# Four graph-attention layers on 128 graphs: score columns become rows by DMA through DRAM instead of by TensorE transposes

## The chip, the cores and the metric

The kernel runs on one core of a Trainium2 chip, as one launch. A core has a matrix engine (TensorE; PE in the profile, with PEld for its weight loads), three engines for elementwise work (VectorE: DVE; ScalarE: ACT; GpSimd: POOL), and a sync engine (SP) that in this kernel issues every DMA. The metric is the device time of one execution in microseconds, lower is better; the median of several executions is compared.

## What is computed

128 independent graphs of 128 nodes with 512 features each go through four graph-attention layers. Each layer first normalizes (layer norm, then ReLU), and adds its result to its input. Cut to what matters:

```python
h = relu(layernorm(x))
# layer 0: scores f1_i + f2_j, f = (h W^T) a;   attention over j of h itself; elu
# layer 1: GAT, 4 heads of 256, x W1, softmax over sources; elu; then a second
#          GAT of 1 head on the 1024 features, W2;            + bias b2
# layer 2: scores h.w_src_i + h.w_dst_j + b;    attention over j of h itself
# layer 3: 8 heads of 64, x W_proj, scores a_src_i + a_dst_j + b;  relu
x = x + layer(h)
# in every layer and head:
e[i, j] = leaky_relu(own[i] + other[j], 0.2)      # masked where adj has no edge
att     = softmax(e)
```

So a graph has five attentions with 1, 4, 1, 1 and 8 heads: 15 score matrices of 128 x 128. Each is the sum of a column (`own`, one value per partition) and of a row (`other`, one value per free position). Both are computed as columns, with nodes on the partitions, so `other` has to be turned into a row that every partition holds.

## The kernel before, in words

All is float32. Weights are loaded once and stay in SBUF (`w1x`, `w2x`, `wpx`: the projection weights with the score vectors folded in as leading columns, lines 85 to 94 and 129 to 171; pool `setup` holds what only this preparation needs). Then each graph is a Python generator, `graph` (L422), which makes three masks from the adjacency, runs `layer0` to `layer3` one after the other, and stores its 128 x 512 tile `xt`. Every `yield` is a place where the next graph may come in. The loop at L445 keeps up to FLYING = 7 graphs in flight, steps each of them by one yield per turn, and starts a new graph every APART = 11 turns at the earliest. A graph before the change has 71 turns. The input of a graph is loaded two graphs ahead (`loaded`, L411).

The kernel is written for a tile framework. It places the waits between engines, and it also decides in which order the instructions of different graphs stand on an engine: this order is near the program's, with exceptions, and is fixed when the program is built. Each engine takes its own list in that order. In the built programs, one pitch of this list (one graph starts, one ends, all seven in flight advance) repeats unchanged through the middle of the run.

The pieces the change and the prediction touch:

- `norm_relu` (L177): `bn_stats` and `bn_aggr` on DVE (L180, L182), epsilon and the power -0.5 on POOL (L185, L187), `nmr` on DVE (L190), and `h` on ACT (L192). Four times a graph.
- `dot` (L196): score columns of layers 0 and 2, one DVE instruction of 128 x 512 for each.
- `projected` (L278): matmuls of `ht` or `y` against a weight, in column parts, each part copied from PSUM by ACT (L293). The score columns are the first columns of the first part.
- `transposed` (L210): TensorE transposes, four to a bank (L217), copied out by ACT (L219).
- `attention` (L223): for each head a TensorE transpose of the `other` column, broadcast to 128 columns, into PSUM (L233): this is the row on all partitions. Then on DVE, for each head, row plus mask with the maximum along the row (L240), the shift (`neg`, `nm`), the addition of `own` (L257 or L259) and the leaky ReLU (L262); on ACT the exponential with its sum, one instruction for each head (L266); on DVE the reciprocal `rz` (L275).
- `applied` (L295): transpose of the weights, and one matmul of 128 x 512 (L299).
- The multi-head attentions have their own matmuls (L337 with output `po`, L393 with output `pa`). The transposed mask of layer 1 is a TensorE transpose too (L433).

SP carries, before the change, only loads of `xt` and of adjacencies (one for four graphs) and the stores of results, L415, L419 and L439.

Of the kernel before, what the change touches and what calls it, by code (L numbers as in the profile page):

```python
# [8 lines left out]
F32 = mybir.dt.float32  # L9
I32 = mybir.dt.int32  # L10
AF = mybir.ActivationFunctionType
ALU = mybir.AluOpType
# [4 lines left out]
LOWEST = -3.0e38  # L17
SLOPE = 0.2
EPS = 1e-5
FLYING = 7  # L20
APART = 11
AHEAD = 2

# [2 lines left out]
def kernel(  # L26
# [23 lines left out]
    nc = tc.nc  # L50
    B, P, D = x.shape
    KC = D // P
    H1, F1 = l1_src1.shape
    HF = H1 * F1
    FC = HF // P
    H3 = l3_watt.shape[0]
# [2 lines left out]


    const = ctx.enter_context(tc.tile_pool(name="const", bufs=1))
    adjp = ctx.enter_context(tc.tile_pool(name="adjp", bufs=3))
    xpool = ctx.enter_context(tc.tile_pool(name="xpool", bufs=FLYING + AHEAD))
    masks = ctx.enter_context(tc.tile_pool(name="masks", bufs=FLYING))
    big = ctx.enter_context(tc.tile_pool(name="big", bufs=2))
    mid = ctx.enter_context(tc.tile_pool(name="mid", bufs=3))
    small = ctx.enter_context(tc.tile_pool(name="small", bufs=8))
    ps = ctx.enter_context(tc.tile_pool(name="ps", bufs=8, space=PSUM))

    def bank(name):  # L70
        return ps.tile([P, 512], F32, tag="bank", name=name)
# [40 lines left out]
    with tc.tile_pool(name="setup", bufs=1) as st:  # L112
# [47 lines left out]
        for c in range(KC):  # L160
            for s in range(2):
# [8 lines left out]
                    wpx[:, c, s * H3 : (s + 1) * H3], prod, AX.X, ALU.add  # L170
                )

# [44 lines left out]
        yield  # L220
        return r

    def attention(own, other, mask, nh, tag):  # L223


        e = (big if nh > 4 else mid).tile([P, nh, P], F32, tag=tag, name=tag)
        mx = small.tile([P, nh], F32, tag=f"mx{nh}", name="mx")
        for g in range(0, nh, 4):
            m = min(4, nh - g)
            pb = bank("pb")  # L230
            for j in range(m):

                nc.tensor.transpose(  # L233
                    pb[:, j * P : (j + 1) * P],
                    other[:, g + j : g + j + 1].to_broadcast([P, P]),
                    ident,
                )
            yield
            for j in range(m):
                nc.vector.tensor_tensor_reduce(  # L240
                    out=e[:, g + j, :],
                    in0=pb[:, j * P : (j + 1) * P],
                    in1=mask,
                    scale=1.0,
                    scalar=LOWEST,
                    op0=ALU.add,
                    op1=ALU.max,
                    accum_out=mx[:, g + j : g + j + 1],
                )

        neg = small.tile([P, nh], F32, tag=f"neg{nh}", name="neg")
        nc.vector.scalar_tensor_tensor(neg, mx, -1.0, own, ALU.mult, ALU.subtract)
        nm = small.tile([P, nh], F32, tag=f"nm{nh}", name="nm")
        nc.vector.scalar_tensor_tensor(nm, neg, SLOPE, neg, ALU.mult, ALU.min)
        ef = e.rearrange("p h q -> p (h q)")
        if nh == 1:
            nc.vector.tensor_scalar(ef, ef, own, None, ALU.add)  # L257
        else:
            nc.vector.tensor_tensor(  # L259
                e, e, own.unsqueeze(2).to_broadcast([P, nh, P]), ALU.add  # L260
            )
        nc.vector.scalar_tensor_tensor(ef, ef, SLOPE, ef, ALU.mult, ALU.max)  # L262
        yield
        z = small.tile([P, nh], F32, tag=f"z{nh}", name="z")
        for j in range(nh):
            nc.scalar.activation(  # L266
                e[:, j, :],
                e[:, j, :],
                AF.Exp,
                bias=nm[:, j : j + 1],  # L270
                accum_out=z[:, j : j + 1],
            )
        yield
        rz = small.tile([P, nh], F32, tag=f"rz{nh}", name="rz")
        nc.vector.reciprocal(rz, z)  # L275
        return e, rz

    def projected(lhs, n_k, w, parts, to):  # L278

        width = w.shape[2] // parts  # L280
        for lo in range(0, w.shape[2], width):
            pm = bank("pm")
            for c in range(n_k):
                nc.tensor.matmul(  # L284
                    pm[:, :width],
                    lhsT=lhs[:, c, :],
                    rhs=w[:, c, lo : lo + width],
                    start=(c == 0),
                    stop=(c == n_k - 1),
                )  # L290
                if c % 4 == 3:
                    yield
            nc.scalar.copy(to[:, lo : lo + width], pm[:, :width])  # L293

    def applied(e, values):  # L295

# [7 lines left out]
    def layer0(xt, mask):  # L304
        h = yield from norm_relu(xt)
        f = small.tile([P, 2], F32, tag="f0", name="f0")
        dot(h, u1, f[:, 0:1])
        dot(h, u2, f[:, 1:2])
        yield
        e, rz = yield from attention(f[:, 0:1], f[:, 1:2], mask, 1, "e0")  # L310
        pa = yield from applied(e, h)

        t = mid.tile([P, D], F32, tag="t0", name="t0", bufs=2)
        nc.scalar.activation(t, pa, AF.Exp, scale=rz)
        yield
        nc.vector.tensor_scalar(t, t, 1.0, -1.0, ALU.min, ALU.add)
        nc.vector.scalar_tensor_tensor(t, pa, rz, t, ALU.mult, ALU.max)
        yield
        nc.gpsimd.tensor_tensor(xt, xt, t, ALU.add)  # L319
        yield  # L320

    def layer1(xt, mask):
        h = yield from norm_relu(xt)
        nc.gpsimd.tensor_tensor(xt, xt, b2, ALU.add)
        ht = yield from transposed(h.rearrange("p (c q) -> p c q", q=P), KC, "ht")
        fx = big.tile([P, E1 + HF], F32, tag="xl", name="xl")
        yield from projected(ht, KC, w1x, 3, fx)
        xl = fx[:, E1:]
        e, rz = yield from attention(fx[:, H1:E1], fx[:, :H1], mask, H1, "e1")
        nc.vector.tensor_tensor(e, e, rz.unsqueeze(2).to_broadcast([P, H1, P]), ALU.mult)  # L330
        yield
        et = yield from transposed(e, H1, "et1")
        y = big.tile([P, FC, P], F32, tag="y1", name="y1")
        for g in range(0, FC, 4):
            po = bank("po")
            for c in range(g, g + 4):
                nc.tensor.matmul(  # L337
                    po[:, (c - g) * P : (c - g + 1) * P],
                    lhsT=xl[:, c * P : (c + 1) * P],
                    rhs=et[:, c * P // F1, :],  # L340
                    start=True,
                    stop=True,
                )
            yield
            nc.vector.tensor_tensor(
                y[:, g : g + 4, :],
                po.rearrange("p (j q) -> p j q", q=P),
                b1[:, g : g + 4].unsqueeze(2).to_broadcast([P, 4, P]),
                ALU.add,
            )  # L350
        yield
        yf = y.rearrange("p c q -> p (c q)")

        t = big.tile([P, HF], F32, tag="t1", name="t1", bufs=1)
        nc.vector.tensor_scalar(t, yf, 0.0, None, ALU.min)
        yield
        nc.scalar.activation(t, t, AF.Exp)  # L357
        yield
        nc.vector.scalar_tensor_tensor(yf, t, -1.0, yf, ALU.add, ALU.max)  # L359
        yield  # L360
        gx = mid.tile([P, E2 + D], F32, tag="x2", name="x2", bufs=2)
        yield from projected(y, FC, w2x, 2, gx)
        yield
        e, rz = yield from attention(gx[:, 1:2], gx[:, 0:1], mask, 1, "e0")
        pa = yield from applied(e, gx[:, E2:])
        nc.vector.scalar_tensor_tensor(xt, pa, rz, xt, ALU.mult, ALU.add)

    def layer2(xt, mask):
        h = yield from norm_relu(xt)
        f = small.tile([P, 2], F32, tag="f0", name="f2")  # L370
        dot(h, w_src, f[:, 0:1])
        dot(h, w_dst, f[:, 1:2])
        yield
        fb = small.tile([P, 1], F32, tag="fb", name="fb")
        nc.gpsimd.tensor_tensor(fb, f[:, 0:1], b_l2, ALU.add)
        e, rz = yield from attention(fb, f[:, 1:2], mask, 1, "e0")
        pa = yield from applied(e, h)
        nc.vector.scalar_tensor_tensor(xt, pa, rz, xt, ALU.mult, ALU.add)

    def layer3(xt, mask):  # L380
        h = yield from norm_relu(xt)
        ht = yield from transposed(h.rearrange("p (c q) -> p c q", q=P), KC, "ht")
        fx = mid.tile([P, E3 + D], F32, tag="x3", name="x3", bufs=2)
        yield from projected(ht, KC, wpx, 2, fx)
        f, xh = fx[:, :E3], fx[:, E3:]
        yield
        fb = small.tile([P, H3], F32, tag="fb3", name="fb3")
        nc.gpsimd.tensor_tensor(fb, f[:, :H3], b_l3, ALU.add)
        e, rz = yield from attention(fb, f[:, H3:], mask, H3, "e3")
        et = yield from transposed(e, H3, "et3")  # L390
        pa = bank("pa")
        for k in range(H3):
# [109 lines left out]
```

## Time and profile before

| | |
|---|---|
| runs | 3704.16, 3705.19, 3707.38 us; median 3705.19 us |
| profiled execution | 3706.62 us, of which the span is 3704.8 us |
| PE busy | 3606.2 us, 97% |
| DVE busy | 3075.8 us, 83% |
| ACT busy | 2131.2 us, 58% |
| POOL busy | 982.2 us, 27% |
| moved by DMA | 88.54 MB, 24 GB/s on average |
| from 500 to 3000 us | PE 2500.0, DVE 2131.0, ACT 1490.7, POOL 687.0 us busy of 2500 |
| stores of results issued | first at 191.2 us, last at 3701.7 us |

The span runs from the first to the last instruction of the core; about 1.8 us of the time lie around it. A group of the profile is a line of the kernel with its tiles; "mean ns" is the length of one instruction, from its start to the end of its write. On DVE and ACT the next instruction often starts before this one's end, so the distance between two starts, read from the timeline, is shorter than the mean (for L240: 280 ns long, 210 ns apart), and the distance is what an engine can do in a row. A float32 matmul or transpose is two instructions in the counts of PE. Ends on PE are modelled, so a busy share of 97% alone does not say that PE works all the time; that it never waits is read from the list of waits.

The kernel's life has three parts: about 57 us in which weights are prepared, a ramp until seven graphs are in flight, and then a steady state in which every pitch looks like the one before.

### The profile page before, as it was taken

What the parts mean: (1) busy time and instruction counts of PE and PEld (TensorE: products, weight loads), DVE (VectorE), ACT (ScalarE), POOL (GpSimd) and SP (SyncE); (2) the same over time, 40 slices, a digit from 0 to 9 for tenths busy, and PEclk for the clock granted to TensorE, in tenths of its full rate; (3) what the DMA queues carried; (4) which work ended last, traced back from release to release, by engine and by line L of the source; (5) the groups of instructions that cost most, each with busy time, mean ns of one, the idle gap of its engine ahead of it and who ended that gap; (6) DMA issues with size and microseconds to landing.
All of it is one profiled execution on the core that took longest, in us unless ns stands there. A gap on an engine that the chain in (4) does not pass through costs nothing.

```text
span 3704.8 us, 60130 instructions
## 1 busy us (share of the span) xinstructions
PE 3606.2 (97%) x19088; PEld 2870.7 (77%) x19088; DVE 3075.8 (83%) x11634; ACT 2131.2 (58%) x6531; POOL 982.2 (27%) x1671
## 2 busy tenths in 40 slices
PE   2999999999999999999999999999999999999997
PEld 1787787788788788788788788788788788778785
DVE  5788888888888888888888888888888888888884
ACT  1455655665565565565665665565565565565563
POOL 1222222222222222222222222232232222222220
PEclk7999999999999999999999999999999999999997
DMA  4000000000000000000000000000000000000000
GB/s 136 4 21 24 21 24 24 21 21 24 21 21 27 21 18 27 21 21 26 21 18 26 21 21 27 21 18 27 21 21 27 20 19 26 21 18 23 16 9 15
DMA packets 60238, 88.54 MB, mean 24 GB/s; under 512 B 7185, under 2 KB 23569, under 8 KB 59921
## 3 DMA queue, kind: packets, MB, share of 16 engines
q1 hardware_dynamic: 59920, 84.70, 6.9%
q8 instruction: 151, 2.47, 0.3%
q14 instruction: 167, 1.36, 0.1%
HBM read 51.13 MB, written 33.55 MB: 23 GB/s over the span
## 4 chain that ended last, share of the span: by engine, by line
PE 96%; DVE 2%; DMA 1%; ACT 1%; POOL 0%; issue 0%; SPq 0%; DVEq 0%; ACTq 0%; POOLq 0%
PE pm L284 60%; PE pt L217 9%; PE pa L299 9%; PE po L337 6%; PE pa L393 6%; PE pb L233 6%; DMA wpx<-in_L_gnn_W_proj_dram 0%; PE ptm L433 0%; ACT e L266 0%; DVE junk L134 0%; DVE st L180 0%; DVE junk L148 0%; DVE e L240 0%; DVE e L262 0%; DVE e L259 0%
## 5 line engine op out<-in xcount | busy, mean ns | idle before, releaser
L266 ACT ACTIVATE e<-e,nm 128x128 f32<-128x128 f32 x1920 | 750.0, 392 | 500.8 <-DVE e L262 494.1
L284 PE MATMUL pm<-w2x,y 128*128 128x257 f32 x4096 | 980.5, 382 | 0.0
L284 PE MATMUL pm<-w1x,ht 128*128 128x344 f32 x3072 | 953.8, 453 | 0.5 <-ACT ht L219 0.5
L284 PEld LDWEIGHTS pm<-w2x,y 128*128 128x128 f32 x4096 | 737.4, 190 | 85.5 <-issue 0.2
L284 PEld LDWEIGHTS pm<-w1x,ht 128*128 128x128 f32 x3072 | 565.1, 191 | 292.7 <-issue 63.1
L319 POOL TENSOR_TENSOR xt<-xt,t 128x512 f32<-128x512 f32 x128 | 163.7, 1279 | 1610.6 <-DVE mv L182 1535.7
L192 ACT ACTIVATE h<-xt,nmr,rstd 128x512 f32<-128x512 f32 x512 | 401.5, 807 | 198.9 <-DVE nmr L190 195.3
L284 PE MATMUL pm<-wpx,ht 128*128 128x264 f32 x2048 | 495.0, 388 | 0.0
L240 DVE CUSTOM_DVE_ANT_0 e<-pb,m 128x128 f32<-128x128 f32 x1920 | 461.6, 280 | 18.2 <-PE pb L233 17.9
L284 PEld LDWEIGHTS pm<-wpx,ht 128*128 128x128 f32 x2048 | 371.9, 192 | 61.9 <-issue 0.2
L217 PE MATMUL pt<-ident,e 128*128 128x128 f32 x1920 | 342.5, 276 | 31.9 <-ACT e L266 21.1
L219 ACT COPY et<-pt 128x128 f32<-128x128 f32 (+1 forms) x768 | 323.4, 421 | 73.3 <-PE pt L217 64.9
L266 ACT ACTIVATION_READ_ACCUMULATOR e<-e,nm 128x1 f32 x1920 | 358.5, 187 | 0.0
L187 POOL TENSOR_TENSOR rstd<-ve,minus_half 128x1 f32<-128x1 f32 x512 | 343.9, 672 | 42.6
L262 DVE SCALAR_TENSOR_TENSOR e<-e 128x128 f32<-128x128 f32 (+2 forms) x640 | 353.8, 553 | 0.0
L180 DVE BATCH_NORM_STATS2 st<-xt 128x6 f32<-128x512 f32 x512 | 342.5, 669 | 3.9 <-POOL xt L319 3.9
L293 ACT COPY x<-pm 128x257 f32<-128x257 f32 (+1 forms) x512 | 184.5, 360 | 269.5 <-PE pm L284 269.2
L293 ACT COPY xl<-pm 128x344 f32<-128x344 f32 x384 | 165.8, 432 | 273.6 <-PE pm L284 273.4
L217 PEld LDWEIGHTS pt<-ident,e 128*128 128x128 f32 x1920 | 243.4, 141 | 68.2 <-ACT e L266 29.2
L359 DVE SCALAR_TENSOR_TENSOR y<-t,y 128x1024 f32<-128x1024 f32 x128 | 156.8, 1225 | 141.3 <-ACT t L357 141.3
L337 PE MATMUL po<-et,xl 128*128 128x128 f32 x2048 | 272.2, 276 | 1.3 <-ACT et L219 1.3
L337 PEld LDWEIGHTS po<-et,xl 128*128 128x128 f32 x2048 | 250.2, 193 | 12.8 <-ACT et L219 2.2
(74 smaller groups left out, 5264.6 us busy)
## 6 DMA issues: line engine op xcount, KB each, us to landing
xt<-in_x_dram SPq DMA_DIRECT2D x128, 256.0 KB, 2.6
out_dram<-xt SPq DMA_DIRECT2D x128, 256.0 KB, 2.0
at<-in_adj_dram SPq DMA_DIRECT2D x32, 256.0 KB, 2.8
w1x<-in_L_gnn_W_dram SPq DMA_DIRECT2D x1, 2048.0 KB, 8.2
w2x<-in_L_gnn_W_dram SPq DMA_DIRECT2D x1, 2048.0 KB, 13.9
wpx<-in_L_gnn_W_proj_dram SPq DMA_DIRECT2D x1, 1024.0 KB, 16.1
w<-in_L_gnn_W_dram SPq DMA_DIRECT2D x1, 1024.0 KB, 9.6
ab<-in_L_gnn_att_src_dram SPq DMA_DIRECT2D x1, 512.0 KB, 4.9
```

The source lines that it names most:

```text
L180: nc.vector.bn_stats(st6, xt)
L187: nc.gpsimd.tensor_tensor(rstd, ve, minus_half, ALU.pow)
L192: nc.scalar.activation(h, xt, AF.Relu, bias=nmr, scale=rstd)
L217: nc.tensor.transpose(pt[:, j * P : (j + 1) * P], t[:, g + j, :], ident)
L219: nc.scalar.copy(r[:, g : g + m, :].rearrange("p m q -> p (m q)"), pt[:, : m * P])
L240: nc.vector.tensor_tensor_reduce(out=e[:, g + j, :], in0=pb[:, j * P : (j + 1) * P], in1=mask, scale=1.0, scalar=LOWEST, op0=ALU.add, op1= ...
L262: nc.vector.scalar_tensor_tensor(ef, ef, SLOPE, ef, ALU.mult, ALU.max)
L266: nc.scalar.activation(e[:, j, :], e[:, j, :], AF.Exp, bias=nm[:, j : j + 1], accum_out=z[:, j : j + 1],)
L284: nc.tensor.matmul(pm[:, :width], lhsT=lhs[:, c, :], rhs=w[:, c, lo : lo + width], start=(c == 0), stop=(c == n_k - 1),)
L293: nc.scalar.copy(to[:, lo : lo + width], pm[:, :width])
L299: nc.tensor.matmul(pa, lhsT=et[:, 0, :], rhs=values, start=True, stop=True)
L337: nc.tensor.matmul(po[:, (c - g) * P : (c - g + 1) * P], lhsT=xl[:, c * P : (c + 1) * P], rhs=et[:, c * P // F1, :], start=True, stop=True,)
```

## The change

The transposes of score columns in `attention` go. In their place, `as_rows` writes the `n` columns from SBUF to a DRAM scratch `r` of n x 128 values, and `on_partitions` reads `r` back into `rb`, 128 partitions with all n rows each. Both are DMAs on SP. `attention` then reads `rb` in SBUF where it read PSUM. Between the write and the read stand WRITTEN = 2 yields, between the read and the first use READ = 2 yields; in `projected` the write is issued right after the copy of the first column part, and the remaining parts stand in the place of those two yields. The pools that the graphs use are opened after the preparation of the weights, where they were opened before it, so their memory may be the one that `setup` gave back. FLYING goes from 7 to 9, and with it the number of `xt` and mask buffers. A graph has 78 turns instead of 71.

```diff
-FLYING = 7
+FLYING = 9
+WRITTEN, READ = 2, 2
...
+    dram = ctx.enter_context(tc.tile_pool(name="dram", bufs=4, space=bass.MemoryType.DRAM))
...
-    adjp = ctx.enter_context(tc.tile_pool(name="adjp", bufs=3))
-    xpool = ctx.enter_context(tc.tile_pool(name="xpool", bufs=FLYING + AHEAD))
-    masks = ctx.enter_context(tc.tile_pool(name="masks", bufs=FLYING))
-    big = ctx.enter_context(tc.tile_pool(name="big", bufs=2))
-    mid = ctx.enter_context(tc.tile_pool(name="mid", bufs=3))
-    small = ctx.enter_context(tc.tile_pool(name="small", bufs=8))
     ps = ctx.enter_context(tc.tile_pool(name="ps", bufs=8, space=PSUM))
...
                     wpx[:, c, s * H3 : (s + 1) * H3], prod, AX.X, ALU.add
                 )
 
+    adjp = ctx.enter_context(tc.tile_pool(name="adjp", bufs=3))
+    xpool = ctx.enter_context(tc.tile_pool(name="xpool", bufs=FLYING + AHEAD))
+    masks = ctx.enter_context(tc.tile_pool(name="masks", bufs=FLYING))
+    big = ctx.enter_context(tc.tile_pool(name="big", bufs=2))
+    rows = ctx.enter_context(tc.tile_pool(name="rows", bufs=2))
+    mid = ctx.enter_context(tc.tile_pool(name="mid", bufs=3))
+    small = ctx.enter_context(tc.tile_pool(name="small", bufs=8))
...
-    def attention(own, other, mask, nh, tag):
+    def as_rows(cols, n):
+
+        r = dram.tile([n, P], F32, tag=f"r{n}", name="r")
+        with nc.allow_non_contiguous_dma(reason="a column of scores becomes a row"):
+            nc.sync.dma_start(out=r.rearrange("h p -> p h"), in_=cols)
+        return r
+
+    def on_partitions(r, n):
+        t = rows.tile([P, n, P], F32, tag=f"rb{n}", name="rb")
+        nc.sync.dma_start(
+            out=t.rearrange("p h q -> p (h q)"),
+            in_=r.rearrange("h q -> (h q)").partition_broadcast(P),
+        )
+        return t
+
+    def attention(own, rb, mask, nh, tag):
...
-        for g in range(0, nh, 4):
-            m = min(4, nh - g)
-            pb = bank("pb")
-            for j in range(m):
-
-                nc.tensor.transpose(
-                    pb[:, j * P : (j + 1) * P],
-                    other[:, g + j : g + j + 1].to_broadcast([P, P]),
-                    ident,
-                )
-            yield
-            for j in range(m):
-                nc.vector.tensor_tensor_reduce(
-                    out=e[:, g + j, :],
-                    in0=pb[:, j * P : (j + 1) * P],
...
+        for j in range(nh):
+            nc.vector.tensor_tensor_reduce(
+                out=e[:, j, :],
+                in0=rb[:, j, :],
...
+    def spread(cols, n):
+
+        r = as_rows(cols, n)
+        for _ in range(WRITTEN):
+            yield
+        rb = on_partitions(r, n)
+        for _ in range(READ):
+            yield
+        return rb
+
-    def projected(lhs, n_k, w, parts, to):
+    def projected(lhs, n_k, w, parts, to, cols):
...
             nc.scalar.copy(to[:, lo : lo + width], pm[:, :width])
+            if lo == 0:
+                r = as_rows(cols, cols.shape[1])
+        yield
+        rb = on_partitions(r, cols.shape[1])
+        for _ in range(READ):
+            yield
+        return rb
...
     def layer0(xt, mask):
...
-        yield
-        e, rz = yield from attention(f[:, 0:1], f[:, 1:2], mask, 1, "e0")
+        rb = yield from spread(f[:, 1:2], 1)
+        e, rz = yield from attention(f[:, 0:1], rb, mask, 1, "e0")
     def layer1(xt, mask):
...
-        yield from projected(ht, KC, w1x, 3, fx)
+        rb = yield from projected(ht, KC, w1x, 3, fx, fx[:, :H1])
...
-        yield from projected(y, FC, w2x, 2, gx)
-        yield
+        rb = yield from projected(y, FC, w2x, 2, gx, gx[:, 0:1])
     def layer2(xt, mask):
...
-        yield
...
+        rb = yield from spread(f[:, 1:2], 1)
     def layer3(xt, mask):
...
-        yield from projected(ht, KC, wpx, 2, fx)
+        rb = yield from projected(ht, KC, wpx, 2, fx, fx[:, H3:E3])
-        yield
```

## The prediction

> **What bounds the kernel now.** I read the page's engine shares and its chain first, then the list of waits, then the timeline of a steady pitch, to see which engine never waits. The chain of work that ended last:
>
> ```profile
> PE 96%; DVE 2%; DMA 1%; ACT 1%; POOL 0%; issue 0%; SPq 0%; DVEq 0%; ACTq 0%; POOLq 0%
> PE pm L284 60%; PE pt L217 9%; PE pa L299 9%; PE po L337 6%; PE pa L393 6%; PE pb L233 6%; DMA wpx<-in_L_gnn_W_proj_dram 0%; PE ptm L433 0%; ACT e L266 0%; DVE junk L134 0%; DVE st L180 0%; DVE junk L148 0%; DVE e L240 0%; DVE e L262 0%; DVE e L259 0%
> ```
>
> PE is the bound, and 6% of it are the transposes (pb, L233) that go. PE's timeline, one pitch apart:
>
> ```profile
> 1002.22 0.27 PE L233 MATMUL pb<-ident,x 128*128 128x128 f32 x1
> ...
> 1004.66 0.60 PE L233 MATMUL pb<-ident,x 128*128 128x128 f32 x4
> 1005.10 0.27 PE L217 MATMUL pt<-ident,e 128*128 128x128 f32 x1
> ...
> 1030.08 0.27 PE L233 MATMUL pb<-ident,x 128*128 128x128 f32 x1
> ```
>
> The same instruction returns after 27.86 us: the pitch. Four transposes take 1005.10 - 1004.66 = 0.44 us, 0.109 each. 128 x 27.86 = 3566 us; the other 139 us of the span are preparation, ramp and drain. Next, who waits:
>
> ```profile
> POOL xt L319 <- DVE mv L182: 1535.7, 121, 13.9
> ...
> DVE nmr L190 <- POOL rstd L187: 150.2, 262, 1.0
> DVE rz L275 <- ACT e L266: 147.0, 255, 3.3
> ...
> DVE y L359 <- ACT t L357: 141.3, 126, 1.2
> ```
>
> PE is not among the large ones. DVE waits some 4.1 us a pitch (sum of its gaps from 500 to 3000 us), mostly for an answer of ACT or POOL to its own last instruction: that belongs to the order of instructions, not to PE. So DVE works 27.9 - 4.1 = 23.7 us of a pitch in a row. Last, how ACT and DVE hand over:
>
> ```profile
> 1011.62 1.22 DVE L262 SCALAR_TENSOR_TENSOR e<-e 128x1024 f32<-128x1024 f32 x1
> ```
> ```profile
> 1012.87 0.40 ACT L266 ACTIVATE e<-e,nm 128x128 f32<-128x128 f32 x1 [0.74 <-DVE e L262]
> 1013.18 0.19 ACT L266 ACTIVATION_READ_ACCUMULATOR e<-e,nm 128x1 f32 x1
> 1013.27 0.39 ACT L266 ACTIVATE e<-e,nm 128x128 f32<-128x128 f32 x1
> ```
>
> ACT starts 0.03 us after DVE's end; one exponential follows another every 0.39 us, so eight take 3.2 us.
>
> **What the Trainium skill says.** "DMA: Bandwidth & Descriptors", Anatomy of one DMA, puts a fixed cost of about 2 us on a DMA, most of it the receipt of the write. The trace agrees: 256 KB stores land after 2.0 us, loads after 2.6 us. The same page, Rules for kernel authors: a strided last dimension becomes one descriptor per element, and a DMA that reads what another wrote must wait for its semaphore. The trace before has element-wise loads only at the start, and no such pair. "Perfetto Trace Analysis", Tensor Engine Instruction, calls ACT, DVE and GpSimd "strict FIFO"; the waits above agree. My argument rests on it.
>
> **The change part by part.**
>
> *Transposes removed.* 15 x 0.109 = 1.63 us a pitch, leaving PE 26.23: 209 us in all if PE stays the bound.
>
> *L240 reads SBUF.* Its starts are 0.21 us apart from PSUM; L262 on the same shape, from SBUF, 0.20. No change, hidden by nothing; at worst 15 x 0.02 = 0.3 us on DVE.
>
> *DMAs.* A pitch gets five writes (15 x 128 = 1920 four-byte elements) and five reads (15 x 64 KB = 0.98 MB; a 256 KB store moves in 0.85 us, so 3.3 us of all 16 engines). SP's list per pitch is: write f2, read f2, write xl, write f0, read xl, store, read f0, load, write x3, read x3, write x2, read x2. Ten issues of 0.35 to 0.43 us are 4 us of SP. Every read waits for its write, and the load for the store; behind them stands the rest of this list. Neither bandwidth nor SP is near its limit.
>
> *One round trip.* A write is a store of 2.0 us less its 0.85 of packets plus 0.1: 1.25 us at least, 2 us by the skill's fixed cost, and perhaps 4 if small writes are slow, which no row shows. I take 1.6. A one-row read: a load of 2.6, less 0.95, plus 0.25: 1.9 us. Four rows 2.65, eight rows (512 KB) 3.05. Below nothing isn't possible: nobody waited for the transposes long (17.9 us in all).
>
> *FLYING, pools.* 78 turns over 11 are 7.1 graphs: the limit of 9 is never reached, cost nothing. The first loads now wait for the preparation on DVE (ends 56.7 us): 4 us once. The first graph's five round trips have nothing beside them: 5 x 3.3 = 16 us once. Together 20 us.
>
> *The order.* Built, the changed kernel has another order of instructions on each engine, again one repeating pitch, and each engine must follow it. So I followed its waits once around with the durations above. Time 0: end of the leaky ReLU of the eight heads (layer 3).
> - ACT: eight exponentials to 3.2. Then its list stands: h (0.76), copy et3 (0.54), h (0.76), copy x2 (0.28), et1, ht, et3 (0.54 each), et0 (0.25), ht (0.54), a one-head exponential (0.49), h of the new graph's layer 0 (0.76): 6.0 in a row, to 9.2. PE has its inputs by then.
> - DVE has meanwhile done two `bn_stats`, waited for POOL (1.33 us from `bn_aggr` to `nmr`, as at 1021.69 to 1023.02), and done the dots of layer 2 by 7.3; it then waits for that last h. Dots of layer 0: to 10.45.
> - DVE: f2's attention 0.6, layer 3's product 0.8, leaky ReLU 0.3, sum into xt 1.1, bias 0.65, small ones 0.3, minimum 0.65: 14.85. ACT's exponential of t and the way back: 15.97. y 1.15, elu of layer 0 and a head of e1 1.25: 18.4. POOL's addition 1.28 and `bn_stats` 0.6, e1's leaky ReLU 0.6: 21.0.
> - ACT: four exponentials of e1 with three copies between: 23.5. DVE: rz and scaling of e1 0.85: 24.35. Eight L240: 26.05. xt 0.65, neg to `bn_stats` 1.9, leaky ReLU 1.22: 29.8.
>
> So the ring closes after 29.8 us, over PE's 26.23. DMA waits lie on it as follows. f2: dots end 7.3, write and read 1.6 + 1.9 and hand-overs 0.1: 10.9, against 10.45: **0.4 us exposed**, and behind it on DVE the whole list above. xl: copied at 9.85, rows at 14.2 against 14.85: hidden by layer 3's end. x3: copied 17.4, its rows by 23 against 24.35: hidden by e1's softmax. x2 and f0 are early by 3 us and more. If the cover goes, each adds what it is late.
>
> Pitch 29.8 + 0.4 = 30.2; 128 x 30.2 = 3866; plus 139 and 20: span 4025. The profiled execution before has 1.8 us around its span (3706.6, against a median of 3705.2): **4025 us**. Late next are DVE and ACT waiting for each other; PE idles about 4 us a pitch.
>
> **Rivals.**
> 1. *PE stays the bound.* If the framework's order leaves the ring some slack that I missed, at 26.2 or less, PE sets the pitch: 3706.6 - 209 + 20 = 3518 us, faster. It decides where the ring is 3.6 us shorter than I added up, for instance if the h of layer 0 need not stand behind eight exponentials. For it: PE now has 96% of the chain, DVE has only 23.7 us of work. Against: each of those steps is fixed by a list. Chance 0.12.
> 2. *The ring about equals the old pitch*, some 27.7: 3706. Chance 0.04.
> 3. *Small writes are slow*: at 4.5 us a write, f2's rows come at 7.3 + 6.5 = 13.8, 3.35 late: pitch 33.15, 128 x 33.15 + 159 + 2 = 4404 us. For it: 4-byte elements; against: the preparation's element-wise loads pass 744 packets of 4 bytes in half a microsecond. Chance 0.12.
>
> **How the numbers follow.** The ring as added up, 0.72: 4025, from 3855 (pitch 28.9, if each of some 18 hand-overs is 0.05 too long) to 4285 (write of 3.6 us: pitch 32.2). The range reaches a little into rivals 2 and 3: 3830 to 4330; outside stay rivals 1 and 2 and the far half of 3. About 0.2% (7.4 us) is what measurement can tell from no change. Faster: rival 1, 0.12, and a third of rival 2, 0.01. Same: 0.02. Slower: 0.85.
>
> **What would show it.** Steady stores should be about 30.2 us apart, PE should idle near 4 us a pitch, and the chain should pass from PE to DVE and ACT, with L266 and L192 on it. DVE should wait for `rb` of f2 about 0.4 us a pitch, and hardly for other rows; write issues should land within 1.3 to 2 us. I am wrong on the ring if PE has no gaps and the stores are 26.2 apart; wrong on the size if `rb` holds DVE for microseconds a pitch.

## The result, and the profile after

The changed kernel takes 7232.6 us (median of four runs, 7219.2 to 7242.1); the kernel before took 3706.3 us beside it (3704.2 to 3707.5). The ratio is 1.951, with a 95% interval from 1.948 to 1.955. The forecast had the direction, slower, but said 4025 us: the loss is 3526 us where 319 were expected.

The page of the changed kernel, its engine shares, the chain of work that ended last, and the costliest group of DVE:

```profile
PE 4120.9 (57%) x17168; PEld 3018.6 (42%) x17168; DVE 3182.8 (44%) x11634; ACT 2039.2 (28%) x6531; POOL 996.3 (14%) x1671
...
DMA 66%; DVE 15%; PE 13%; ACT 4%; issue 1%; SPq 1%; POOL 0%; DVEq 0%; ACTq 0%
...
L249 DVE CUSTOM_DVE_ANT_0 e<-rb,m 128x128 f32<-128x128 f32 x1920 | 473.0, 292 | 3478.5 <-DMA rb<-r 3478.5
```

Before, the chain was 96% PE. Now two thirds of it are DMAs, and no engine is busy for more than 57% of the span. L249 is the old L240, the first reader of the rows: it works 473 us, as before (461.6), but stands 3478.5 us waiting for `rb`. That wait alone is about the size of the loss.

The DMA issues of the changed kernel (KB of one, then the median time from issue to landing in us):

```profile
out_dram<-xt SPq DMA_DIRECT2D x128, 256.0 KB, 5.2
rb<-r SPq DMA_DIRECT2D x384, 64.0 KB, 4.9
...
r<-f SPq DMA_DIRECT2D x256, 0.5 KB, 8.6
...
r<-xl SPq DMA_DIRECT2D x128, 2.0 KB, 11.5
r<-x SPq DMA_DIRECT2D x128, 0.5 KB, 7.6
```

A write of one score column, 512 bytes in all, lands after 8.6 (f) or 7.6 us (x2, the last line), where 1.6 was taken. The smallest transfer is among the slowest. The 8.6 is the middle of two kinds, as the landings one by one show: the writes of f2 have no other write ahead of them and land after 7.8 us, those of f0 are issued 0.5 us behind the write of xl and land after 11.2. A read of one row lands after 4.9 us (taken: 1.9), and even the store of 256 KB, which the change did not touch, went from 2.0 to 5.2 us.

SP's timeline shows what these do to one pitch (start, length of the issue):

```profile
3005.93 0.32 SPq L231 DMA_DIRECT2D r<-f  x1
3013.96 0.32 SPq L236 DMA_DIRECT2D rb<-r  x1
3014.33 0.43 SPq L231 DMA_DIRECT2D r<-xl  x1
3014.85 0.46 SPq L231 DMA_DIRECT2D r<-f  x1
3025.25 0.32 SPq L236 DMA_DIRECT2D rb<-r  x1
...
3061.77 0.32 SPq L231 DMA_DIRECT2D r<-f  x1
```

And DVE's, its starts that waited for rows (the bracket is the idle time before):

```profile
3019.24 0.29 DVE L249 CUSTOM_DVE_ANT_0 e<-rb,m 128x128 f32<-128x128 f32 x1 [10.47 <-DMA rb<-r]
...
3030.32 0.29 DVE L249 CUSTOM_DVE_ANT_0 e<-rb,m 128x128 f32<-128x128 f32 x1 [7.39 <-DMA rb<-r]
...
3047.47 0.29 DVE L249 CUSTOM_DVE_ANT_0 e<-rb,m 128x128 f32<-128x128 f32 x1 [7.75 <-DMA rb<-r]
...
3059.83 0.29 DVE L249 CUSTOM_DVE_ANT_0 e<-rb,m 128x128 f32<-128x128 f32 x1 [2.22 <-DMA rb<-r]
```

The first write (f2) is issued at 3005.93, its read at 3013.96, 8.0 us later, and DVE goes on at 3019.24: a trip of 13.3 us, priced at 3.6. The trip of xl takes 16.0 us (3014.33 to 3030.32), that of x3 16.2, that of x2 13.3. SP takes its list in order, as the times of issue show, so each read that waits for its write also holds what stands behind it: the write of xl is issued only when the read of f2 has gone. DVE waits 10.47 + 7.39 + 7.75 + 2.22 = 27.8 us for rows in this pitch of 55.8 us. On average of stores 20 to 110 the pitch is 55.25 us (before: 27.86); in the stretch from 1000 to 3000 us PE is busy 1160.4 of 2000 us, and its granted clock is 0.78.

### The profile page after: what moved, and what is told of

It reads as the page before. It is cut to its first block, busy times and chain, and to the rows that moved or that the text cites. A ratio compares the mean times of both kernels' runs of the same rounds, so it can differ in the third digit from the quotient of the medians.

```text
span 7228.1 us, 58423 instructions
## 1 busy us (share of the span) xinstructions
PE 4120.9 (57%) x17168; PEld 3018.6 (42%) x17168; DVE 3182.8 (44%) x11634; ACT 2039.2 (28%) x6531; POOL 996.3 (14%) x1671
## 4 chain that ended last, share of the span: by engine, by line
DMA 66%; DVE 15%; PE 13%; ACT 4%; issue 1%; SPq 1%; POOL 0%; DVEq 0%; ACTq 0%
DMA r<-xl 20%; DMA rb<-r 18%; DMA r<-f 15%; DMA r<-x 14%; PE pm L304 8%; PE pa L326 5%; DVE e L249 2%; DVE junk L203 2%; ACT e L275 2%; DVE nm L263 2%; DVE y L386 2%; DVE st L184 1%; DVE e L271 1%; DVE e L268 1%; DVE t L344 1%; ACT x L313 1%
## 5 line engine op out<-in xcount | busy, mean ns | idle before, releaser
L249 DVE CUSTOM_DVE_ANT_0 e<-rb,m 128x128 f32<-128x128 f32 x1920 | 473.0, 292 | 3478.5 <-DMA rb<-r 3478.5
L326 PE MATMUL pa<-x,et 128*128 128x512 f32 x256 | 264.7, 1137 | 1912.1 <-ACT et L223 1912.1
L304 PE MATMUL pm<-w2x,y 128*128 128x257 f32 x4096 | 1287.5, 462 | 7.1 <-DVE y L386 5.2
L221 PE MATMUL pt<-ident,e 128*128 128x128 f32 x1920 | 509.5, 354 | 1060.7 <-ACT e L275 1014.0
L304 PEld LDWEIGHTS pm<-w2x,y 128*128 128x128 f32 x4096 | 954.3, 244 | 366.2 <-issue 179.5
L326 PEld LDWEIGHTS pa<-x,et 128*128 128x128 f32 x256 | 64.1, 311 | 1943.0 <-ACT et L223 1943.0
L221 PEld LDWEIGHTS pt<-ident,e 128*128 128x128 f32 x1920 | 325.0, 180 | 1242.5 <-ACT e L275 1094.5
L454 POOL TENSOR_SCALAR m<-m 128x128 f32<-128x128 f32 x128 | 114.6, 895 | 2110.7 <-DVE m L453 2051.1
L189 POOL TENSOR_SCALAR ve<-mv 128x1 f32<-128x1 f32 x512 | 116.1, 227 | 1882.2 <-DVE mv L186 1865.3
L346 POOL TENSOR_TENSOR xt<-xt,t 128x512 f32<-128x512 f32 x128 | 214.1, 1673 | 1058.9 <-DVE neg L261 925.6
```

The lines of the kernel that those rows point to most:

```text
L221: nc.tensor.transpose(pt[:, j * P : (j + 1) * P], t[:, g + j, :], ident)
L249: nc.vector.tensor_tensor_reduce(out=e[:, j, :], in0=rb[:, j, :], in1=mask, scale=1.0, scalar=LOWEST, op0=ALU.add, op1=ALU.max, accum_out= ...
L304: nc.tensor.matmul(pm[:, :width], lhsT=lhs[:, c, :], rhs=w[:, c, lo : lo + width], start=(c == 0), stop=(c == n_k - 1),)
L326: nc.tensor.matmul(pa, lhsT=et[:, 0, :], rhs=values, start=True, stop=True)
```

## The experiments

Two theories after the result. A: many small writes into one and the same row of memory wait for each other, so that the landing grows with the number of elements on the row. B: any DMA of 4-byte elements is this slow, wherever they go (or the reads of one row by 128 partitions are what is slow). Apart from these stood the order: is a pitch of some 30 us what remains if trips are quick, and whence does it come? Beside these runs the kernel before took 3705.69 us (3705.36 beside h0, h1, k1 and k2). The runs e1 to e8, h0 and h1 are one execution each, k1 and k2 the median of four.

### The writes and the reads, each alone

In `e1_writes_spread` each element is written to a row of memory of its own; in `e2_reads_spread` each partition reads its own row; `e3_both_spread` has both. The scratch is 128 x n x 128 values, laid out once, and the order of instructions on PE, DVE and ACT stays that of the changed kernel. In these three the rows read don't hold the scores of all nodes, so they measure time alone.

```diff
-            nc.sync.dma_start(out=r.rearrange("h p -> p h"), in_=cols)
+            nc.sync.dma_start(out=r[:, :, 0], in_=cols)
...
-            in_=r.rearrange("h q -> (h q)").partition_broadcast(P),
+            in_=r.rearrange("p h q -> p (h q)"),
```

The first pair of lines is e1 (its read takes `r[0]` for all), the second is e2 (its write goes to `r[0]`), both are e3. `e4_rows_written` goes another way: one TensorE transpose turns the n columns into n rows, ACT copies them, and the DMA writes whole rows.

```diff
-            nc.sync.dma_start(out=r.rearrange("h p -> p h"), in_=cols)
+        pr = bank("pr")
+        nc.tensor.transpose(pr[:n, :P], cols, ident)
+        row = small.tile([n, P], F32, tag=f"row{n}", name="row", bufs=4)
+        nc.scalar.copy(row, pr[:n, :P])
+        nc.sync.dma_start(out=r, in_=row)
```

> The writes of score columns put every 4-byte element on a 512-byte line of its own in the scratch; the reads take the first line as before, so the rows are mostly zeros and the scores are left out. The order of instructions on PE, DVE and ACT is that of the changed kernel. Theory A (128 small writes into one 512-byte line wait for each other): the median write lands in about 2 us in place of 7.3, and the pitch loses about 6 + 8 + 9 us of the three writes on the ring, to 33 us; about 4400 to 4700 us. Theory B (any 4-byte write to DRAM is slow): writes stay at 7 us or more and the time near 7230 us.

> The writes are those of the changed kernel; each partition reads a row of its own from the scratch, in place of all 128 the same one, so the scores are left out. Theory A (128 reads of one row wait for each other): reads of one row land in 2 to 2.5 us in place of 4.9, the pitch loses some 3 us for each of the two to three reads on the ring; 6100 to 6600 us. Theory B (a read is slow because it follows a write, or because of the queue): reads stay near 5 us, and the time near 7230 us.

> Both of the former at once: own lines for the written elements, own rows for the reading partitions; scores left out. Theory A: trips of some 4 us, nearly all hidden but that of f2, so the ring of 29.8 to 31 us that the prediction added up: 3950 to 4200 us, PE idle 4 us a pitch. Rival (the order of instructions leaves more slack than added up): pitch 26.2 to 28 us, 3520 to 3750 us. Rival (DMA latency isn't in the addresses): near 7230 us.

> The column is turned into rows by one TensorE transpose for each attention (5 a graph, where the kernel before had 15), copied out of PSUM by ACT, and written as whole 512-byte rows; the read of one row by all partitions stays. Theory A: writes land in 2 us or a little more, reads stay near 5 us; pitch 37 to 42 us, 4800 to 5500 us. Theory B (any write that a read must wait for costs 7 us and more): near 7000 us.

Measured:

| | time, us | pitch, us | landing of r<-f / r<-xl / rb of 64 KB, us | DVE waits for rb, us |
|---|---|---|---|---|
| after | 7232.6 | 55.25 | 8.6 / 11.5 / 4.9 | 3478.5 |
| e1, writes spread | 4230.05 | 31.85 | 1.7 / 2.2 / 2.8 | 298.3 |
| e2, reads spread | 7124.64 | 54.29 | 8.5 / 13.1 / 3.6 | 3317.4 |
| e3, both | 4148.43 | 31.24 | 1.7 / 2.1 / 1.8 | 147.2 |
| e4, rows written | 4505.84 | 34.16 | not shown | 18.0 |

The time of e3 lies in its expected range. e1 and e4 came out below theirs (4400 to 4700 and 4800 to 5500 us), and e2 lies between its two theories. DMA issues of e1, the same rows as above:

```profile
out_dram<-xt SPq DMA_DIRECT2D x128, 256.0 KB, 3.2
rb<-r SPq DMA_DIRECT2D x384, 64.0 KB, 2.8
...
r<-f SPq DMA_DIRECT2D x256, 0.5 KB, 1.7
...
r<-x SPq DMA_DIRECT2D x128, 0.5 KB, 1.4
```

The same 128 elements of 4 bytes, from the same partitions, on the same list of SP, land after 1.7 us instead of 8.6 (x2, the last line: 1.4 instead of 7.6) when each has a row of its own. So it isn't the size of the elements: B falls. The slow writes, with all that follows from them, are worth 7232.6 - 4230.05 = 3002.6 us; spreading the reads alone gives 108 us, and 82 more after the writes (e1 to e3). What remains from e3 to the kernel before, 4148.43 - 3705.69 = 442.7 us, is no matter of where the bytes go.

The chain of e3 says that with quick trips the engines hand over to each other, and PE no longer has nearly all of it:

```profile
DVE 37%; PE 31%; ACT 15%; DMA 13%; issue 2%; POOL 1%; SPq 0%; DVEq 0%; ACTq 0%
```

e4 recovers 2727 us of the loss by whole rows (DMA is 2% of its chain), but puts a transpose and an ACT copy ahead of each trip and has an order of its own: 34.16 us a pitch, 2.9 more than e3.

### How far apart is far enough

As e1, with the elements 16 or 64 bytes apart instead of 512 (the last size of the scratch is 4 or 16 values; the reads take n x 128 values of it for all). The scores are left out here as well.

> As in the run with spread writes, but written elements 16 bytes apart, so that up to 32 of them share 512 bytes; the reads take one row from the start of the scratch for all partitions, and the scores are left out. If small writes into the same 512 bytes are done one after the other (128 took about 7 us, so 55 ns each), 32 take 1.8 us and a write of one column lands after about 3.1 us; pitch 33 to 36 us, 4400 to 4800 us. If only elements on lines of their own are quick, it stays at 7 to 8 us, and the time near 7200 us.

> The same with written elements 64 bytes apart: 8 in 512 bytes. If writes into the same 512 bytes go one after the other at 55 ns, 8 take 0.4 us: a write of one column lands after about 1.8 us, time 4230 to 4350 us. If only lines of their own are quick, writes stay at 7 to 8 us and the time near 7200 us.

Measured: 4602.14 us at 16 bytes (pitch 34.66) and 4255.38 us at 64 bytes (pitch 32.06). The write of one column, at 16 and then at 64 bytes:

```profile
r<-f SPq DMA_DIRECT2D x256, 0.5 KB, 3.0
...
r<-x SPq DMA_DIRECT2D x128, 0.5 KB, 1.4
```
```profile
r<-f SPq DMA_DIRECT2D x256, 0.5 KB, 2.2
...
r<-x SPq DMA_DIRECT2D x128, 0.5 KB, 1.4
```

Both times lie in their expected ranges. The medians of f alone (8.6, 3.0, 2.2 and 1.7 us for 128, 32, 8 and 1 elements on 512 bytes) look like a fixed price for each further element, but they mix the two kinds of writes. Median landings in us:

| bytes from element to element | 4 (after) | 16 (e5) | 64 (e6) | 512 (e1) |
|---|---|---|---|---|
| x2, one column | 7.6 | 1.4 | 1.4 | 1.4 |
| f2, one column | 7.8 | 1.4 | 1.4 | 1.4 |
| f0, one column, right behind xl | 11.2 | 4.0 | 2.4 | 1.9 |
| xl, four columns | 11.5 | 4.2 | 2.7 | 2.2 |
| x3, eight columns | 10.9 | 6.0 | 3.8 | 3.0 |

A column without another write right ahead of it is slow with its elements side by side and quick at 16 bytes, where 32 of them on 512 bytes land as fast as one. So A does not hold as it was put: the number of elements on a row of 512 bytes does not set the landing, and the 3.0 us of e5 met the expected 3.1 by luck, as the middle of 1.4 and 4.0. What the runs show is that the distance decides: the same elements are slow at 4 bytes apart, and for a lone column 16 are enough. Where more elements are on their way (f0 behind xl, xl, x3), some of the delay is left at 16 bytes and a little at 64. How long the stretch of memory is on which elements meet, and whether they wait for each other there, stays open. More rows cost less than their number: four columns to four rows take 11.5 us and eight to eight rows 10.9, not four or eight times 7.6.

### The rest of the change, alone

`e7_rest_alone` keeps the transposes of before and takes the rest: nine graphs in flight, the pools after the preparation, and 7 more turns ahead of the attentions (two each, one ahead of x2). `e8_rows_for_nothing` has no transposes and no writes; the rows are read from a weight, so that nobody waits for a score on its way (the scores are left out).

```diff
+        yield
+        yield
         e, rz = yield from attention(f[:, 0:1], f[:, 1:2], mask, 1, "e0")
...
-            nc.sync.dma_start(out=r.rearrange("h p -> p h"), in_=cols)
+            pass
...
-            in_=r.rearrange("h q -> (h q)").partition_broadcast(P),
+            in_=l1_w1[:P, : n * P],
```

> The kernel before, transposes and all, with the rest of the change alone: FLYING = 9, the pools opened after the weights are prepared, and the same 78 turns for a graph (seven more yields ahead of the attentions). Theory (the rest costs only a few microseconds at the start): pitch 27.9 us with PE never waiting, 3705 to 3745 us. Rival (more turns alone move instructions so that engines wait for each other): pitch 29 us or more, over 3850 us.

> No columns are written; each attention still gets its rows by a DMA of the same size, but from the weights in DRAM, a row of its own for each partition and with no write to wait for, so the scores are left out. The framework then orders the instructions anew. Theory (the ring of 31 us belongs to the order that the round trips bring about): PE is the bound again, pitch 26.2 to 27.5 us, 3520 to 3680 us. Rival (DVE and ACT wait for each other in any order once the transposes are gone): pitch 29 to 31 us, 3870 to 4120 us.

Measured: e7 4039.58 us with a pitch of 30.53, e8 4151.08 us with a pitch of 31.63. The theory fell in both. e7 lies where its rival put it; e8 is a little above its rival's range too, and as it keeps the seven turns, it doesn't show that the rival holds for any order. The chain and the first waits of e7:

```profile
PE 46%; DVE 27%; ACT 20%; issue 3%; POOL 3%; DMA 0%; SPq 0%; ACTq 0%; DVEq 0%; POOLq 0%
```
```profile
POOL fb L396 <- ACT x L294: 1525.6, 127, 13.8
ACT e L267 <- DVE e L263: 1258.0, 513, 5.1
```

There is no new DMA in this kernel, and yet DVE and ACT wait for each other: ACT stood 494.1 us for the leaky ReLU before (L262), 1258.0 us here. So a ring of waits like the one that the prediction added up needs neither the trips nor the loss of the transposes. The likely cause was the seven turns, and a sharper theory could be tried: a new graph comes every 11 turns, so a turn more or less in one layer moves it against the layers of the other graphs within that round, and the order on the engines with it. Then 11 turns, a whole round, must cost next to nothing. `h1_eleven_turns` has them in one place, ahead of the attention on x2 (with a third buffer for x2), and `h0_nine_flying` has none.

```diff
+        for _ in range(APART):
+            yield
         e, rz = yield from attention(gx[:, 1:2], gx[:, 0:1], mask, 1, "e0")
```

> The kernel before with its transposes, 9 graphs in flight, and 11 turns (one whole round of the 11 turns between two graphs) added at one place, ahead of the attention on x2 in layer 1, instead of the 7 turns at four places of the run of the rest alone (4039.58 us). In the steady state each engine has the order of instructions of the kernel before. Theory (a turn costs nothing by itself; the 7 turns cost 334 us since they move the layers of different graphs against each other inside the round of 11): pitch 27.8 to 28.0 us, TensorE idle under 0.3 us a pitch, and one more round of filling, 28 us: 3733 us (3705 to 3760). Rival (turns, or graphs in flight, cost by their number, 334 / 7 = 48 us each): above 3950 us, pitch above 29.5 us.

> The kernel before with 9 in place of 7 for the graphs in flight and the pools laid after the setup; no turn added, so that no more than 7 graphs are in flight at any time. Theory (the order in the steady state is that of before): 3705 us (3695 to 3730), pitch 27.86 us. Rival (the larger pools or their place cost part of the 334 us): above 3740 us.

Measured: 3719.91 us with eleven more turns, 3708.85 us with none, both with a pitch of 27.86 us. Eleven turns cost 14.6 us once (28 were expected), seven cost 334 us. The chain of the kernel with eleven:

```profile
PE 95%; DVE 2%; ACT 1%; POOL 0%; issue 0%; DMA 0%; SPq 0%; ACTq 0%; POOLq 0%; DVEq 0%
```

PE never waits again (2000.0 of 2000 us busy from 1000 to 3000 us). In the traces of h0 and h1 the lists of PE, ACT and DVE in one pitch are those of before, instruction by instruction; in e7 all three differ. So in these runs the number of turns, the graphs in flight and the pools cost next to nothing, and the order on the engines does. That the place in the round of eleven decides this order fits h1 and e7, but h1 adds turns at one place and e7 at four, and no run adds seven at one.

### Trips far away, with the old places in the round

If that is so, rows by way of memory might gain something where each added step is a whole round and the trip is hidden in it. `k1_far_rows` does this for the two attentions of several heads, 12 of the 15 transposes, with whole rows written as in e4 (and a third buffer for xl and x3); `k2_far_columns` writes columns as in the changed kernel.

```diff
+    def far(cols, n):
+        r = dram.tile([n, P], F32, tag=f"r{n}", name="r")
+        pr = bank("pr")
+        nc.tensor.transpose(pr[:n, :P], cols, ident)
+        yield
+        row = small.tile([n, P], F32, tag=f"row{n}", name="row", bufs=2)
+        nc.scalar.copy(row, pr[:n, :P])
+        nc.sync.dma_start(out=r, in_=row)
+        for _ in range(APART - READ - 1):
+            yield
...
+        rb = yield from far(fx[:, :H1], H1)
+        e, rz = yield from attention(fx[:, H1:E1], rb, mask, H1, "e1")
```

> The kernel before, with the rows of the two attentions of several heads (12 of the 15 transposes of a graph) by way of memory: one transpose of the score columns, a ScalarE copy, whole rows of 512 bytes written, read back by all partitions, and 11 turns added in each of the two layers so that all phases in the round of 11 stay those of before; the read is issued 4 turns (some 10 us) ahead of its use. Theory (TensorE sets the pitch as long as the order is that of before and trips are hidden): 12 transposes less and 2 more at 0.109 us, pitch 27.86 - 1.09 = 26.8 us; 3705 - 127 x 1.09 + 2 more rounds of 26.8 = 3621 us (3580 to 3670). Rival (ScalarE, VectorE or the transfers bind just below the old pitch): 3700 us or more.

> As the run before with rows far away, but the score columns are written as in the changed kernel, 4 bytes each to a row of 512 bytes, with no transpose: 512 and 1024 elements in the two writes of a graph, the read issued 6 turns (some 16 us) after the write. Theory (a slow write costs only where something waits for it: 11 to 13 us of landing are hidden behind 16 us of turns): pitch 27.86 - 12 x 0.109 = 26.55 us, 3705 - 127 x 1.31 + 2 x 26.5 = 3592 us (3560 to 3650), writes still landing after 8 us or more. Rival (the slow writes also hold back loads, stores and reads on the same queues and so the engines): above 3700 us.

Measured: k1 3814.57 us, ratio to before 1.0295 (95% interval 1.028 to 1.0311); k2 5114.29 us, ratio 1.380 (1.378 to 1.383). Both are slower, and the expectation failed twice. The chain of k1:

```profile
DVE 34%; ACT 27%; PE 20%; POOL 12%; issue 4%; DMA 1%; SPq 0%; ACTq 0%; DVEq 0%
```

PE no longer leads it. DVE waits only 135.1 us for rows: the trip is hidden. PE's order is that of before without the twelve transposes (and with the two new ones). But PE now has one wait in each pitch. First PE before, around the first projection of layer 1, then the same place in k1:

```profile
2006.18 0.60 PE L217 MATMUL pt<-ident,h 128*128 128x128 f32 x4
...
2007.62 0.60 PE L233 MATMUL pb<-ident,x 128*128 128x128 f32 x4
...
2008.17 2.48 PE L284 MATMUL pm<-w1x,ht 128*128 128x344 f32 x8
```
```profile
2019.98 0.60 PE L221 MATMUL pt<-ident,h 128*128 128x128 f32 x4
...
2023.42 2.58 PE L307 MATMUL pm<-w1x,ht 128*128 128x344 f32 x8 [1.57 <-ACT ht L223]
```

The reason is on ACT in k1:

```profile
2015.71 0.40 ACT L289 ACTIVATE e<-e,nm 128x128 f32<-128x128 f32 x1 [3.26 <-DVE e L285]
...
2022.41 0.40 ACT L289 ACTIVATE e<-e,nm 128x128 f32<-128x128 f32 x1
...
2022.79 0.57 ACT L223 COPY ht<-pt 128x512 f32<-128x512 f32 x1
```

The copy of `ht` stands behind fifteen exponentials on ACT, and the first of these waited 3.26 us for DVE. The framework had put the exponentials elsewhere on ACT's list, though PE's list was kept; DVE's list differs too. So whole rounds did not keep the order here as they did in h1. Some of the transposes had also filled the gap: before, 0.44 us of `pb` lay between `pt` of `h` and the projection. From 1000 to 3000 us PE is busy 1889.8 us: of the pitch of 28.74 us that is 27.16, and it waits 1.58. So PE's work fell by 0.70 us a pitch, where 1.09 were expected, and the wait is more than either.

In k2 the read, asked for six turns after the write, stands right behind it on SP's list. One pitch of SP:

```profile
2031.80 0.37 SPq L231 DMA_DIRECT2D r<-x  x1
2041.41 0.32 SPq L235 DMA_DIRECT2D rb<-r  x1
2041.82 0.39 SPq L231 DMA_DIRECT2D r<-xl  x1
2051.18 0.32 SPq L235 DMA_DIRECT2D rb<-r  x1
```

Each read is issued 9.4 to 9.6 us after the write ahead of it. Six turns in the program did not put other DMAs between a write and its read on SP; the framework decided that list too. So the slow landing stayed exposed, DVE waited 1376.4 us for rows, and the write of xl was issued only when the read of x3 had gone. The experiment shows that the column writes are still slow when only two are made per graph (10.5 us for xl), but not what they would cost if nobody stood behind them on SP. That wasn't tried.

No run here beats the kernel before.

## Why the prediction was wrong

**The bound, and its removal.** PE was the bound, and with the transposes gone it did not stay the bound: rival 1 (3518 us) didn't come. What the transposes are worth no run shows as forecast; in k1, at about the granted clock of before (0.986 after 0.987), ten fewer took 0.70 us a pitch off PE's busy time, not 1.09. (In PE's counts a transpose is one instruction, 1920 of `pb` for 15 in each of 128 graphs, and a float32 matmul two; so the 0.44 us are four transposes.)

**"One round trip".** This is the step that failed. It took 1.6 us for a write, at most 4; the profile says 8.6 for f, 11.5 for xl, 7.6 for x2 and 10.9 for x3. e1 puts 3002.6 of the 3526 us on this term. The reasoning built a small write from a large store, less its packets: 2.0 - 0.85 + 0.1. The kernel before has no write of single elements, and the price of a write to 128 neighbouring addresses can't be had from a store of 2 KB runs. The fixed cost of about 2 us that the Trainium skill gives ("DMA: Bandwidth & Descriptors", Anatomy of one DMA) is fitted there to DMAs issued from GpSimd, which the prediction passed over; these come from SP. A write whose elements lie apart stays below it (1.4 us for a lone column in e1), and one whose elements lie side by side takes about four times as much (7.6). Two lines of that page pointed the right way and were not used: Specifications says that below 512 bytes a DMA does a read-modify-write, which no run here shows at work, and which alone would not tell elements at 4 bytes (7.6 us) from elements at 16 (1.4); and Rules for kernel authors warns of transposing by a plain DMA with a rearranged pattern, as 19 times slower than the hardware's way. `r.rearrange("h p -> p h")` is such a pattern. The factor itself isn't shown here; 7.6 against 1.4 us is.

**The argument against rival 3** was the second half of the same mistake. It said that 744 packets of 4 bytes passed in half a microsecond. In the changed kernel the packets of the column of f2 pass as quickly, all between 3006.7 and 3007.0 us, about 9 ns each; the landing comes 7 us later. How long these packets are in the trace says nothing on when their write is done. Rival 3 named the right term with too small a price: 4.5 us for 8.6, and for one trip alone where four are exposed.

**The reads.** 1.9 us for one row was right for e3 (1.8). In the changed kernel it was 4.9. Rows of their own alone bring it to 3.6 (e2), quick writes alone to 2.8 (e1): both have a part in it, the slow writes the larger one. (In e1 the row that is read also holds one element just written, where it held 128.)

**"f0, x2, xl, x3 hidden".** Each cover was right in size for trips of 3.6 to 4.7 us (in e3 rows cost DVE 147.2 us in all, 1.2 us a pitch) and far too short for 13 to 16. SP's list, called "not near its limit", is no limit of rate, but its order puts one trip behind another, so that four trips stand in a row in a pitch of 55 us.

**"The order", the ring of 29.8 us.** Right within a few per cent, and in its steps. In the pitch shown of the changed kernel, 55.8 us less 27.8 us of waits for rows leaves 28.0; with quick trips (e3) the pitch is 31.24, where 30.2 was forecast. The difference times 128 is 133 us, and e3 is 123 us over the 4025. In e3's pitch at 2000 us DVE waits 0.42 us for the rows of xl, which had been called hidden by 0.65, and none for those of f2, which had been given 0.4: that the sizes agree is luck. The steps lie where the ring had them. After the leaky ReLU of the eight heads, e3's trace has y at 15.9 us (15.97 forecast), the end of e1's leaky ReLU at 21.4 (21.0) and the start of the eight first readers at 24.6 (24.35). These readers then take 2.9 us, not 1.7.

**"L240 reads SBUF: no change."** This small term was mis-sized too. It held in the changed kernel (473.0 us, after 461.6), where DVE mostly waits, but not with quick trips. The first readers of e3:

```profile
L256 DVE CUSTOM_DVE_ANT_0 e<-rb,m 128x128 f32<-128x128 f32 x1920 | 597.9, 353 | 148.0 <-DMA rb<-r 147.2
```

They cost 136 us more than before, about what e3 lies over the forecast. In its trace 132 of the 1920 take over 0.8 us, each while POOL makes an addition of 128 x 512; before, where they read PSUM, none does. That the two hold each other up fits, but no run parts them.

**"FLYING, pools: cost nothing".** Right for these two (h0: 3708.85), but the sentence passed over the seven turns. Alone, with every transpose kept, they cost 334 us, where e3 is 443 us over the kernel before. The prediction found the ring from the built order, so its sum was not harmed, but it did not see that such a ring comes with the turns alone.

**What would show it.** Stores 55.25 apart, not 30.2; PE idles 23 us a pitch, not 4; DVE waits for `rb` 27 us, not 0.4. "Wrong on the size if `rb` holds DVE for microseconds a pitch" is what came. Two slips in the sums do not matter here: the 4025 us are those of the span, without the 1.8 us around it, and a ring shorter by 18 x 0.05 us gives a pitch of 29.3 with f2's 0.4, not 28.9.

What stays open: why elements side by side land late and on what length of memory they meet, the part of the loss that SP's order has in it (each read held what stood behind it, but no run gave the writes a list of their own), and why the framework puts a read directly behind its write.

## What to carry to other kernels

A transposing DMA that writes single elements side by side has to be priced by a measured landing, not by its bytes, its packets or the landing of a large store; ask how far apart the elements lie, and which writes stand right ahead. And don't draw a law through medians that mix two kinds of writes. In a pipeline of interleaved graphs, compare the order on each engine after adding steps: seven steps changed it and cost 334 us, eleven kept it in h1 and cost 15, and whole rounds did not keep it in k1. And before removing work from the bounding engine, look at which wait it covered: in k1 0.70 us of work went and 1.58 us of waiting came.

## What the runs showed of the hardware that was not expected

- A column of 128 elements of 4 bytes, written to 512 bytes in a row with no write right ahead of it, lands after 7.6 us (x2), and after 1.4 us with the elements 16, 64 or 512 bytes apart (e5, e6, e1). The packets pass in 9 ns each where the landing is slow.
- A write right behind another lands about when that one does: f0 behind xl after 11.2 us, where f2 takes 7.8.
- The store of 256 KB took 5.2 us instead of 2.0 in the changed kernel, 3.2 in e1 and 2.6 in e3. In 104 of the 128 stores after the change no column was on its way, but a read of rows was; in k2, whose column writes are as slow (10.5 us), nothing was beside 124 of the stores, and they landed after 2.0. So the delay goes with the reads beside the store, and grows as these are slower (4.9, 2.8 and 1.8 us for one row).
- 128 partitions that read the same 512 bytes get them after 2.8 us, and after 1.8 us from rows of their own (e1 and e3, 64 KB each).
- TensorE's granted clock was lower in the kernels where it waited much: 0.987 before (97% busy), 0.914 in e5 (82%), 0.893 in k2 (76%), 0.772 after (57%). It does not follow the busy share step by step: 0.988 in e7 (92%), and 0.978 in e3 (86%) but 0.945 in e8 (88%).
